# First stage of an attention block on one core: the depthwise convolution's input as four-row stacks read straight from memory, the value of two images in one column tile, results in 8 KB runs

## The chip, the core and the metric

The program runs on one core of a Trainium2 chip. The core has five engines with their own instruction streams: TensorE (PE, matrix products into PSUM), VectorE (DVE), ScalarE (ACT), GpSimd (POOL) and SyncE (SP, which here only issues transfers). Sixteen DMA engines move data; transfers are issued on a queue of SP, of ACT or of POOL. The metric is the device time of one execution in microseconds; the number quoted is the median of several.

## The reference, cut to what matters

Four layers follow one another on an input of 8 images, 384 channels, 32 x 32 pixels, all in float32. The change concerns only the first part of the first layer.

```python
def _bn(x, g, b):
    m = x.mean(axis=(0, 2, 3), keepdims=True)
    v = x.var(axis=(0, 2, 3), keepdims=True)
    return (x - m) * lax.rsqrt(v + EPS) * g[None, :, None, None] + b[None, :, None, None]

def _dwproj(x, dw, g, b, pw):
    C = x.shape[1]
    y = lax.conv_general_dilated(x, dw, (1, 1), ((1, 1), (1, 1)), feature_group_count=C, ...)
    y = jax.nn.gelu(_bn(y, g, b), approximate=False)
    return jnp.einsum('oc,bchw->bohw', pw, y)
...
q = _dwproj(x, dw_q, g_q, b_q, pw_q).reshape(B, heads, hd, N)
k = _dwproj(x, dw_k, g_k, b_k, pw_k).reshape(B, heads, hd, N)
v = _dwproj(x, dw_v, g_v, b_v, pw_v).reshape(B, heads, hd, N)
attn = jax.nn.softmax(jnp.einsum('bhcn,bhcm->bhnm', q, k) * scale, axis=-1)
```

Ahead of each layer the input is group-normed (12 channels a group). So the first stage computes, for each image, the group norm of x and then three depthwise 3 x 3 convolutions (q, k, v) with zero padding. The batch norm behind them takes its mean and variance over all images, so no attention can start before the convolutions of all eight images have been made and measured.

## The kernel before

The 384 channels are laid out as 128 partitions of 3 chunks (channel 3p + c is chunk c of partition p). An image has 1024 pixels, held as even rows and odd rows, 512 each (`HALF`).

The first stage (`pa`, up to line 534) works in four rounds of two images. The list `PLAN` gives each round eleven work units, each of which fills four PSUM banks and is then handled alike: ACT copies the banks to a result tile `y` (line 502; four such buffers), DVE takes the statistics of its four banks (line 504), and four DMAs, one for each quarter of 32 partitions, store it to DRAM. PE runs in 32 x 32 tiles, sixteen at a time: the row group is a quarter of the channels, the column group `q` one of two images times even or odd rows.

- A `u` unit convolves chunk 2 for one of q, k, v with nine taps from the normed image `xn`, with diagonal 32 x 32 weights `cwd`: 144 matmuls. Its results go by SP to `rawu`.
- An `s` unit takes chunk 0 or 1 of 32 channels from a stack tile `stk`, in which eight channels and four neighbouring rows share 32 partitions. Three taps along the row suffice, since the weights `cws` hold the three taps across rows. The 32 columns are q and k for even and odd outputs, or v with half of the columns unused: 48 matmuls for a pair. Its results go by POOL to `raws`.

The stack tiles are built from the normed image by `stack` (line 384): eight DMAs a tile on SP, with the four row offsets going to every fourth partition.

`norm(k)` makes the group norm of round k: DVE statistics of the two images (line 310), a matmul with `g4` that averages over the group, a second one for the spread of the means, a power on POOL for the inverse root (line 96), and the application by ACT (line 350), for one of the first two images by DVE (line 348), into a new tile `xn` with even and odd rows apart. `todo` puts the steps of round k + 1 among the units of round k. Images are loaded by `load_x`, the first on SP and ACT, the others on POOL.

With the last units, `spread_stacked` and `spread_scale` turn the statistics into scale and shift (through the matmuls `pmove` and `pfs`), and `gelu_image` applies them to q and k of image 0, which `load_b(0)` has fetched back. The scale of v comes last, at line 534. Then the attention stage begins (`pb`): its first matmul is the projection `pq` at line 638, and a memset of the value tiles `vt` (line 586) that stands behind the last scale. The order of instructions on each engine is set by a scheduler, from the order of the program text and the data that each needs.

Of the kernel before, what the change touches and what calls it, by code (L numbers as in the profile page):

```python
# [14 lines left out]
P = 128  # L15
# [6 lines left out]
NSTK = 4  # L22
# [31 lines left out]
def tile_kernel(ctx: ExitStack, tc: tile.TileContext, i: dict, out: bass.AP):  # L54
# [157 lines left out]
    raws = dram.tile([B, 2, 2, 16, 32, HALF], F32, name="raws")  # L212
    rawu = dram.tile([B, 3, 2, P, HALF], F32, name="rawu")
# [5 lines left out]
    def fetch_raw(g, v, rs, ru):  # L219

        for c in range(KC - 1):
            for e in range(2):
                k = 16 * (v % 2) + 8 * e
                nc.sync.dma_start(
                    out=g[:, c, e * HALF : (e + 1) * HALF], in_=rs[c, v // 2, :, k : k + 8, :]
                )
        nc.sync.dma_start(
            out=g[:, KC - 1, :].rearrange("p (e n) -> p e n", e=2),
            in_=ru.rearrange("e p n -> p e n"),
        )  # L230

    def load_b(b):
        acts[b] = {}
        for v in (2, 1, 0):
            acts[b][v] = image(f"g{v}_{b}")
            fetch_raw(acts[b][v], v, raws[b], rawu[b, v])
# [19 lines left out]
    with ExitStack() as pa:  # L256
        wa = pa.enter_context(tc.tile_pool(name="a_w", bufs=1))
        xa = pa.enter_context(tc.tile_pool(name="a_x", bufs=4))
        ya = pa.enter_context(tc.tile_pool(name="a_y", bufs=4))
        sa = pa.enter_context(tc.tile_pool(name="a_s", bufs=2))  # L260

        NK = B // 2
        last = NK - 1
        xts, xns = {}, {}

        def load_x(b, queue):
            xts[b] = image(f"xa{b}")
            load_image(xts[b], x_img[b], queue)

        load_x(0, nc.sync)  # L270
        load_x(1, nc.scalar)
        stk = [wa.tile([P, 2, 2, HALF], F32, name=f"stk{s}") for s in range(NSTK)]
        for t in stk:
            nc.gpsimd.memset(t, 0.0)
        g4 = const.tile([P, P], F32, name="g4_sb")
        nc.gpsimd.dma_start(out=g4, in_=i["g4"])
        cwd = wa.tile([P, 3, 9, 32], F32, name="cwd_sb")
        nc.gpsimd.dma_start(out=cwd, in_=i["cwd"])
        cws = wa.tile([P, 2, 4, 2, 3, 32], F32, name="cws_sb")
        nc.gpsimd.dma_start(out=cws, in_=i["cws"])  # L280
        ident = const.tile([P, P], F32, name="ident_sb")
        sels = wa.tile([P, P], F32, name="sels_sb")
        isv = wa.tile([P, 3], F32, name="isv_sb")
        msk = wa.tile([P, 16], F32, name="msk_sb")
        quad = wa.tile([P, 32], F32, name="quad_sb")

        def load_late():
            for t, nm in (
                (ident, "ident"), (sels, "sels"), (isv, "isv"), (msk, "msk"), (quad, "quad"),
                (gb0, "gb0"), *zip(w_in, ("wq0", "wk0", "wv0")),  # L290
            ):
                nc.gpsimd.dma_start(out=t, in_=i[nm])

        sst = wa.tile([P, 2, 16, NK, 6], F32, name="sst")
        smv = wa.tile([P, 2, 16, 2], F32, name="smv")
        fss = wa.tile([P, 3, 2, 2], F32, name="fss")
        cst = wa.tile([P, 3, 4, NK, 6], F32, name="cst")
        zmv = wa.tile([P, 3, 2, 4], F32, name="zmv")

        def norm(k):  # L300

            xt, state = [xts.pop(2 * k + j) for j in range(2)], {}
            st = sa.tile([P, 2, 2 * KC, 6], F32, tag="gp_st", name=f"gst{k}")
            mv = sa.tile([P, 2, 2], F32, tag="gp_mv", name=f"gmv{k}")
            xns[k] = [xa.tile([P, KC, N], F32, tag="xn", name=f"xn{k}_{j}") for j in range(2)]

            def begin(j):
                for m in range(2 * KC):
                    c, h = divmod(m, 2)
                    nc.vector.bn_stats(st[:, j, m, :], xt[j][:, c, h * HALF : (h + 1) * HALF])  # L310
                nc.vector.bn_aggr(mv[:, j, :], st[:, j].rearrange("p a b -> p (a b)"))

            def middle():
                pg = bank(f"gpa{k}")
                nc.tensor.matmul(
                    pg[:, 0:4], lhsT=g4, rhs=mv.rearrange("p j s -> p (j s)"),
                    start=True, stop=True,
                )
                ga = sa.tile([P, 2, 2], F32, tag="gp_ga", name=f"gga{k}")
                nc.vector.tensor_copy(ga.rearrange("p j s -> p (j s)"), pg[:, 0:4])  # L320
                dm = sa.tile([P, 2], F32, tag="gp_dm", name=f"gdm{k}")
                nc.vector.tensor_tensor(dm, mv[:, :, 0], ga[:, :, 0], ALU.subtract)
# [3 lines left out]
            def end():  # L326
                ga, dm = state["ga"], state["dm"]
                pb = bank(f"gpb{k}")
                nc.tensor.matmul(pb[:, 0:2], lhsT=g4, rhs=dm, start=True, stop=True)
                ve = sa.tile([P, 2], F32, tag="gp_ve", name=f"gve{k}")  # L330
                nc.vector.scalar_tensor_tensor(
                    ve, pb[:, 0:2], 1e-5, ga[:, :, 1], ALU.add, ALU.add
                )
                ss = sa.tile([P, 2, 2], F32, tag="gp_ss", name=f"gss{k}")
                rsqrt(ss[:, 0, :], ve, 2)
# [5 lines left out]
            def apply(c):  # L341
                ss = state["ss"]
                for j in range(2):
                    d = rows_of(xns[k][j][:, c, :], 0, H)
                    x = xt[j][:, c, :].rearrange("p (h e w) -> p h e w", e=2, w=W)
                    sc, sh = ss[:, 0, j : j + 1], ss[:, 1, j : j + 1]
                    if k == 0 and j == 1:
                        nc.vector.tensor_scalar(d, x, sc, sh, ALU.mult, ALU.add)
# [100 lines left out]
        for f in norm(0):  # L449
            f()  # L450
        normed.add(0)
        quads = [slice(32 * r, 32 * r + 32) for r in range(4)]
        for n, (k, kind, g, c) in enumerate(work):
            for k2, f in todo.get(n, ()):
                if f == 0:
                    steps[k2] = norm(k2)
# [1608 lines left out]
```

## Time and profile before

| | us |
|---|---|
| median of 3 runs | 3612.69 |
| lowest and highest | 3610.12, 3613.4 |
| the profiled execution | 3622.18 |
| its span, from the first to the last instruction | 3620.4 |
| PE busy | 3456.4 (95%) |
| DVE busy | 1664.5 (46%) |
| ACT busy | 1285.1 (35%) |
| POOL busy | 271.6 (8%) |
| mean granted TensorE clock | 0.979 |

The page gives busy time of each engine, a row of forty equal slices (a digit is tenths of the slice), DMA queues, the chain of work that ended last, and groups of equal instructions with the idle time ahead of them and what ended it. Other views of the trace list groups, waits or a timeline of a window, or give busy time, granted clock, DMA share and GB/s for stretches chosen by the reader. In a line of stretches the columns are: stretch, its length, busy time and instruction count of PE, PE's weight loads, DVE, ACT and POOL, then clock, DMA share and GB/s. A matmul of float32 leaves two records in the trace. The page's first slice covers 90.5 us, so the first stage takes nearly four slices.

### The profile page before, as it was taken

To read this page: it belongs to the slowest core of one execution; us is meant where nothing else is said; L and a number is where in the kernel's file an instruction comes from. 1 tells how busy PE (TensorE), PEld (TensorE's weight loads), DVE (VectorE), ACT (ScalarE), POOL (GpSimd) and SP (SyncE) were. 2 spreads that over 40 slices of the span, in tenths; PEclk is the share of its full clock that TensorE was granted. 3 is DMA by queue.
4 is the path that set the end of the run, shared out by engine and by line. 5 is a ranking of instruction groups with operands and counts; after the bars stand their busy time and mean duration, and the time that the engine had idled before them with its cause. 6 is when DMAs were issued, how large, how long until landed. Compare 5 with 4: busy or idle time off the path is not lost.

```text
span 3620.4 us, 50244 instructions
## 1 busy us (share of the span) xinstructions
PE 3456.4 (95%) x21323; PEld 1535.1 (42%) x21323; DVE 1664.5 (46%) x2766; ACT 1285.1 (35%) x1517; POOL 271.6 (8%) x310
## 2 busy tenths in 40 slices
PE   5877999999999999999899999999999999999897
PEld 3545343434343434344344534444344444444433
DVE  6434223232323232333346566465764647556663
ACT  3333444444454444444212331323322232322222
POOL 4212000000000000000000010200102010010112
PEclk9988999999999999999999999999999999999898
DMA  8785112121212121211521110110101001010000
GB/s 301 199 228 150 41 48 73 31 77 26 76 26 76 27 75 36 66 49 57 220 110 41 34 38 21 48 38 34 38 34 50 24 34 45 26 53 20 0 34 20
DMA packets 98151, 237.58 MB, mean 66 GB/s; under 512 B 16648, under 2 KB 20984, under 8 KB 97658
## 3 DMA queue, kind: packets, MB, share of 16 engines
q1 hardware_dynamic: 84954, 193.23, 16.9%
q0 software_dynamic: 11664, 37.84, 3.6%
q8 instruction: 172, 2.82, 0.3%
q10 hardware_dynamic: 1296, 3.15, 0.2%
q14 instruction: 65, 0.53, 0.0%
HBM read 132.89 MB, written 75.59 MB: 58 GB/s over the span
## 4 chain that ended last, share of the span: by engine, by line
PE 40%; DVE 9%; ACT 1%; DMA 1%; POOL 0%; issue 0%; DVEq 0%; ACTq 0%; POOLq 0%
PE y L1405 12%; PE ph L1384 9%; DVE y L1480 5%; PE pq L1525 3%; PE pw L1488 3%; PE pf L1832 3%; PE s L1703 2%; PE pav L1729 2%; DVE hd L1370 1%; DMA o<-o 1%; PE pk L1678 1%; PE pv L1687 1%; PE xsb L1664 1%; PE plog L1134 1%; PE pss L1742 1%; DVE off L1595 1%
## 5 line engine op out<-in xcount | busy, mean ns | idle before, releaser
L731 ACT ACTIVATE p<-s 128x1024 f32<-128x1024 f32 x512 | 497.0, 1022 | 365.2 <-PE s L724 364.7
L739 PE MATMUL pav<-p,vt 64*64 64x512 f32 x4096 | 494.4, 588 | 0.0
L1405 PE MATMUL y<-hd,w_sb 128*128 128x512 f32 x1080 | 488.7, 600 | 3.5 <-DVE hd L1370 3.5
L1384 PE MATMUL ph<-h,w_sb 128*128 128x512 f32 x1104 | 486.8, 595 | 5.0 <-ACT h L1333 5.0
L724 PE MATMUL s<-qk,qk 48*64 48x512 f32 x3072 | 370.5, 592 | 0.0
L1384 PEld LDWEIGHTS ph<-h,w_sb 128*128 128x128 f32 x1104 | 207.0, 190 | 266.2 <-issue 250.0
L1405 PEld LDWEIGHTS y<-hd,w_sb 128*128 128x128 f32 x1080 | 199.9, 191 | 248.2 <-issue 235.6
L739 PEld LDWEIGHTS pav<-p,vt 64*64 64x64 f32 x4096 | 167.4, 133 | 274.7 <-issue 274.3
L700 DVE COPY ta<-pav 128x512 f32<-128x512 f32 (+1 forms) x65 | 44.3, 682 | 475.2 <-PE pav L739 475.2
L1480 DVE SCALAR_TENSOR_TENSOR y<-h,tap,y 128x961 f32<-128x961 f32 (+1 forms) x192 | 235.0, 1250 | 0.6
L1394 ACT ACTIVATE hd<-ph,b_sb 128x512 f32<-128x512 f32 x180 | 122.9, 683 | 312.2 <-PE ph L1384 312.2
L1595 DVE SCALAR_TENSOR_TENSOR off<-q,dw_sb,off 128x225 f32<-128x225 f32 (+3 forms) x432 | 212.7, 552 | 1.6
L724 PEld LDWEIGHTS s<-qk,qk 48*64 48x64 f32 x3072 | 113.0, 133 | 221.2 <-issue 198.7
L492 PE MATMUL pk<-xn,cwd_sb 32*32 32x496 f32 (+3 forms) x3456 | 138.3, 632 | 29.2 <-issue 17.3
L502 ACT COPY y<-pk 128x1024 f32<-128x1024 f32 (+1 forms) x132 | 87.1, 740 | 193.6 <-issue 73.7
L1720 ACT ACTIVATE p<-s 128x1024 f32<-128x1024 f32 x96 | 96.2, 1024 | 166.4 <-PE s L1703 142.2
L79 DVE COPY qk<-pq 128x512 f32<-128x512 f32 x48 | 33.2, 692 | 262.0 <-PE pq L638 262.0
L1370 DVE TENSOR_TENSOR hd<-hd,cb 128x512 f32<-128x512 f32 x180 | 123.5, 691 | 40.9 <-ACT hd L1394 40.7
L492 PE MATMUL pk<-stk,cws_sb 32*32 32x496 f32 (+1 forms) x3072 | 124.9, 629 | 17.5 <-issue 11.4
L1765 POOL TENSOR_TENSOR p<-p,p 128x1024 f32<-128x1024 f32 x48 | 113.0, 2355 | 349.6 <-ACT p L1720 349.6
L1488 PE MATMUL pw<-y,upw 128*128 128x512 f32 x288 | 129.6, 603 | 4.4 <-DVE y L1480 4.4
L638 PE MATMUL pq<-g,wq_sb 128*128 128x512 f32 x288 | 130.3, 603 | 0.0
(306 smaller groups left out, 3910.3 us busy)
## 6 DMA issues: line engine op xcount, KB each, us to landing
g<-raws SPq DMA_DIRECT2D x96, 256.0 KB
raws<-y POOLq DMA_DIRECT2D x64, 256.0 KB, 6.9
rawu<-y SPq DMA_DIRECT2D x48, 256.0 KB
g<-rawu SPq DMA_DIRECT2D x24, 512.0 KB
xh<-in_x_dram SPq DMA_DIRECT2D x48, 256.0 KB
f<-in_x_dram SPq DMA_DIRECT2D x24, 512.0 KB
f<-o SPq DMA_DIRECT2D x24, 512.0 KB
o<-ot SPq DMA_DIRECT2D x42, 256.0 KB
```

Of the source, the lines that this page charges most:

```text
L492: nc.tensor.matmul(to[:, r0:r1, c0:c1], lhsT=cwd[rs, g, t, :] if kind == "u" else cws[rs, c, g, e, t, :], rhs=src[rs, r0 + d : r1 + d, c0 ...
L638: nc.tensor.matmul(pq, lhsT=w_in[v][:, c, pr * P : (pr + 1) * P], rhs=rows_of(acts[b][v][:, c, :], h * H // 2, (h + 1) * H // 2) if v == 0 ...
L724: nc.tensor.matmul(s[64 * k : 64 * k + 64, j * HALF : (j + 1) * HALF], lhsT=kt[r, k0 : k0 + 64], rhs=qt[r, h * HALF : (h + 1) * HALF], sta ...
L731: nc.scalar.activation(p, s, AF.Exp, scale=scale)
L739: nc.tensor.matmul(pav[k][64 * j : 64 * j + 64, :], lhsT=vts[b % 2][r, kc, 2 * hd : 2 * hd + 2, :].rearrange("p a b -> p (a b)"), rhs=p[r, ...
L1370: nc.vector.tensor_tensor(hd, hd, state["cb"], ALU.mult)
L1384: nc.tensor.matmul(ph, lhsT=w1[:, e, c, dc * P : (dc + 1) * P], rhs=state["h1"][c], start=(c == 0), stop=(c == KC - 1),)
L1394: nc.scalar.activation(hd, ph, AF.Relu, bias=b1[:, k : k + 1])
L1405: nc.tensor.matmul(y, lhsT=w2[:, e, dc, m * P : (m + 1) * P], rhs=state[h, k], start=(k == 0), stop=(k == NE * KC - 1),)
L1480: nc.vector.scalar_tensor_tensor(d, f, tap2[:, c, t : t + 1], d, ALU.mult, ALU.add)
L1488: nc.tensor.matmul(pw[h], lhsT=upw2[:, c, m * P : (m + 1) * P], rhs=y[c][:, hs], start=(c == 0), stop=(c == KC - 1),)
L1595: nc.vector.scalar_tensor_tensor(d, f, dw3[:, t : t + 1], d, ALU.mult, ALU.add)
```

## The change

- The input comes as a second DRAM array, `xs`, whose layout on the host keeps even and odd rows of each channel apart and has one row of zeros at either end. From it `load_half` reads tiles of four-row stacks of all three chunks: a tile holds half an image, that is two of the four groups of 32 channels, in each chunk, and comes in four DMAs (one a row offset) of 32 partitions, each partition a run of 12 KB. Two neighbouring row offsets of a stack come from the same memory shifted by one image row, so each row is read twice. There are sixteen such tiles, the first four loaded on SP and ACT, all others on SP, in pieces spread over the work units.
- `norm(k)` takes its statistics from the stacks (24 for two images, where there were 12) with a mask `gs4` that counts each row once, and applies scale and shift in place; POOL then multiplies the first and last row of each piece by 0 or 1 (`mrow`), since the padding must stay zero.
- The units: six `a` units a round (q and k, one chunk and two groups of 32 channels, two images: 48 matmuls), and three `v` units (one chunk, all groups), in which two images share one column tile: six passes, three an image, with the weights of the other image's columns zero (96 matmuls).
- Results go by SP to `rqk` and `rv` in an order that makes each partition's run 8 KB. `fetch_raw` reads them back in six DMAs a tensor instead of five.
- The moments of x that the attention stage needs (`xmv`) are made from the stack statistics, which `x_moments` first moves with eight DMAs of 24-byte runs.
- Scale and shift of q and k are made in the last round after its sixth unit (`spread_qk`), those of v at the end (`spread_v`).
- In this stage the engines keep the order of the program text (`manual_schedule`).

The diff, cut:

```diff
-    raws = dram.tile([B, 2, 2, 16, 32, HALF], F32, name="raws")
-    rawu = dram.tile([B, 3, 2, P, HALF], F32, name="rawu")
+    rqk = dram.tile([B, KC, 32, 16, HALF], F32, name="rqk")
+    rv = dram.tile([KC, B, 16, 16, HALF], F32, name="rv")
...
+            src = rw[c, 8 * e : 8 * e + 8] if v == 2 else rq[c, 16 * v + 8 * e :][:8]
+            nc.sync.dma_start(
+                out=g[:, c, e * HALF : (e + 1) * HALF], in_=src.rearrange("q a n -> a q n")
+            )
...
-        xa = pa.enter_context(tc.tile_pool(name="a_x", bufs=4))
+        xa = pa.enter_context(tc.tile_pool(name="a_x", bufs=6))
...
+        pa.enter_context(tc.manual_schedule(engines=set(ENGINES)))
...
+        IN_IM = (0, 1, 2, 3, 4, 11, 12)
+
+        def load_half(m, queue):
+            b, h = divmod(m, 2)
+            t = (
+                image(f"xs{m}") if m in IN_IM
+                else xa.tile([P, KC, N], F32, tag="xs", name=f"xs{m}")
+            )
...
+            def part(d):
+                w = KC * N
+                s = W + (0 if d in (1, 2) else W if d == 3 else -W)
+                src = i["xs"][s : s + B * C * N].rearrange("(b e m n) -> b e m n", b=B, e=2, m=32)
+                queue.dma_start(
+                    out=t.rearrange("p c n -> p (c n)")[d::4],
+                    in_=src[b, 1 - d % 2, :, h * w : (h + 1) * w],
+                )
...
+        for m in range(4):
+            for f in load_half(m, (nc.sync, nc.scalar)[m % 2]):
+                f()
...
+            def begin(j, h):
+                for g in (2 * h, 2 * h + 1):
+                    for c in range(KC):
+                        nc.vector.bn_stats(
+                            xst[:, g, 2 * k + j, c, :], xt[j][h][:, g % 2 * KC + c, :]
+                        )
...
+            def apply(g):
+                ss, h = state["ss"], g // 2
                 for j in range(2):
...
+                    d = xt[j][h][:, g % 2 * KC : g % 2 * KC + KC, :]
...
                     if k == 0 and j == 1:
+                        nc.vector.tensor_scalar(d, d, sc, sh, ALU.mult, ALU.add)
                     else:
+                        nc.scalar.activation(d, d, AF.Identity, bias=sh, scale=sc)
+                    for e, row in enumerate((0, HALF - W)):
+                        f = d[:, :, row : row + W]
+                        nc.gpsimd.tensor_tensor(
+                            f, f, mrow[:, e : e + 1].unsqueeze(2).to_broadcast([P, KC, W]),
+                            ALU.mult,
+                        )
...
-            "s00 s01 s10 u0 s11 s20 s21 u1 s30 s31 u2",
+        PLAN = ["a00 a10 v0 a01 a11 v1 a02 a12 v2"] * last + ["a00 a10 a01 a11 a02 a12 v0 v1 v2"]
...
+        AT = (0, 0, 1, 2, 3, 4, 5, 6, 7, 8), (0, 3, 3, 4, 5, 6, 6, 7, 7, 8)
...
+        def x_moments():
+            for g in range(4):
+                for e in range(2):
+                    nc.sync.dma_start(
+                        out=xnst.rearrange("p b c e s -> p (b c) e s")[32 * g : 32 * g + 32, :, e],
+                        in_=xst[e + 1 :: 4, g].rearrange("p b c s -> p (b c) s"),
+                    )
...
+            if at == 0:
+                for m in ((8, 9, 10, 11), (12,), (13, 14, 15), ())[k]:
+                    loads += load_half(m, nc.sync)
...
+                for a, f in zip(AT[k + 2 > last], norm(k + 1) if k < last else ()):
+                    steps.setdefault(a, []).append(f)
+            for _ in range(2 if k == 0 else 4):
+                if loads and (k > 0 or at > 1):
+                    loads.pop(0)()
...
+            passes = [(j, x) for j in range(2 if kind == "v" else 1) for x in (1, 0, 2)]
...
+                    if kind == "v":
+                        g, w = q, slice(48 - 16 * j, 80 - 16 * j)
                     else:
+                        (u, j), w = divmod(q, 2), slice(0, 32)
+                        g = 2 * s + u
+                    src = halves_of[4 * k + 2 * j + g // 2][:, g % 2 * KC + c, :]
...
                         nc.tensor.matmul(
+                            banks[r][quads[q]].rearrange("p (h w) -> p h w", w=W)[:, :, c0:c1],
+                            lhsT=cws[rs, c, g, x, w], rhs=src[rs, :, c0 + x - 1 : c1 + x - 1],
+                            start=(p == passes[0]), stop=(p == passes[-1]),
                         )
...
+                    nc.sync.dma_start(
+                        out=rqk[2 * k + j, c, :, 4 * g : 4 * g + 4, :], in_=y[quads[q]]
                     )
...
+        spread_v()
+        scales = scale_of(2, fv)
```

## The prediction

> **What bounds the kernel now.** I read the page's slices first, then the windows around the seam between the first stage and the attention stage, then groups, waits and the timeline at that seam.
>
> ```profile
> PE   5877999999999999999899999999999999999897
> PEclk9988999999999999999999999999999999999898
> DMA  8785112121212121211521110110101001010000
> ...
> 0.00:348.66 348.66, 252.79 (x6563) 157.27 (x6564) 157.45 (x355) 120.56 (x161) 96.11 (x172) 0.90 0.77 223
> 348.66:1700.00 1351.34, 1351.34 (x9154) 540.69 (x9158) 411.43 (x674) 640.95 (x654) 8.29 (x5) 1.00 0.19 53
> ```
>
> TensorE (PE) is busy 1351.34 of 1351.34 us after the seam, with no gap in which lost or won time could hide: what the first stage saves, the kernel saves. Only its 348.66 us, with PE busy 252.79, are in play. Two more answers say what fills them.
>
> ```profile
> 99.15:108.57 9.42, 9.42 (x289) 6.40 (x275) 7.11 (x12) 5.91 (x8) 3.09 (x6) 1.00 0.77 169
> ...
> 44.00:60.00 16.00, 6.84 (x162) 2.79 (x144) 14.47 (x31) 2.71 (x5) 5.58 (x11) 0.91 1.02 373
> ...
> 100.00:200.00 100.00, 80.55 (x2163) 49.91 (x2139) 40.59 (x71) 39.25 (x56) 26.03 (x49) 0.91 0.82 214
> ...
> 322.50:326.00 3.50, 3.30 (x98) 1.95 (x76) 3.43 (x12) 2.25 (x5) 1.00 (x2) 1.00 1.00 239
> ...
> L492 PE MATMUL pk<-xn,cwd_sb 32*32 32x496 f32 (+3 forms) x3456 | 138.3, 632 | 29.2 <-issue 17.3 <-ACT y L502 8.9 <-ACT xn L350 3.0
> L492 PE MATMUL pk<-stk,cws_sb 32*32 32x496 f32 (+1 forms) x3072 | 124.9, 629 | 17.5 <-issue 11.4 <-ACT y L502 6.1
> ...
> L504 DVE BATCH_NORM_STATS2 sst<-y 128x6 f32<-128x512 f32 x128 | 78.1, 679 | 54.9 <-ACT y L502 54.7
> ...
> ACT y L502 <- DMA rawu<-y: 49.5, 4, 17.8
> ```
>
> See four things. First, 99.15 to 108.57 is three undisturbed stacked units (96 records each, two per matmul): 3.14 us a unit, 32.7 ns a record. All 6528 records at that rate are 213 us; the rest is waiting. Second, the longest single cause named is ACT's copy waiting for the result buffer `y` until its store has left (49.5 us in 4 waits). Third, DMA: 373 GB/s in 44 to 60, where loads dominate, but 214 over 100 to 200. Fourth, 322.50 to 326.00 is a window where only result stores run, from the SP queue, with all engines full (1.00) at 239 GB/s. So a store out of a 32-partition quarter of `y` runs at 239 GB/s, a load at nearer 400.
>
> **The change part by part.**
>
> PE. Nine-tap chunk-2 units (432 matmuls a round) and stacked units (384) become six q/k units of 48 and three value units of 96: 576 against 816, in four rounds 4608 records against 6528. At 32.7 ns: 151 us of PE instead of 213. At the slower rate of the last nine-tap units (11.14 us between the copies that start at 308.44 and 319.58, for 288 records: 38.7 ns) the value half would add 14 us. The zero columns that let two images share a value tile cost nothing[...]. From the scale matmul on, PE's instruction order is the same in both programs.
>
> DVE. A round has 36 statistics of `y` (44 before) and 24 of the input (12 before), since each row stands in two stack partitions: 60 at 0.68 us plus 8 aggregates at about 0.3 are 43 us a round. Four rounds less the first input, read before PE starts, are 154; with the last round's aggregates (36 x 0.22 and 24 x 0.19, 12.5), four applies of 1.2 and some 3 for the scale steps, DVE needs about 175 us after PE's start: longer than PE.
>
> ACT. Copies are 2 us a unit, 72 in all. The norm in place is 28 activations of 128x1536; from 1.24 us for 128x1024 in the row of L350, 1.85 each, 52 us. With two GELU images, 131 us: covered by DVE's 175. If an apply waits for its scale, the copies queued behind it on ACT wait, and PE with them; two units of PSUM absorb some 6 us.
>
> POOL. It loses 128 result issues and 7 us of memsets and gains 64 edge-row multiplications of 128x96. From 0.557 us at 128x144 and 0.707 at 128x192 (the `wt` multiplications), a straight line gives 0.41 each, 26 us in all, beside other work except the first. Its power of 8 columns takes 1.64 us (row of `rs`) instead of 0.72.
>
> DMA and queues. Gone: 128 stacking copies (16 MB, 0.61 us of SP each). The input is read twice over: 25.2 MB against 12.6, in 12 KB rows. Results stay 37.7 MB, but all 144 stores now go through SP beside the loads, the fetch of image 0 (18 DMAs, 4.7 MB) and eight small copies of 24-byte runs, and in the program's order each waits for the DMA eight before it on the SP and ACT queues. Two hundred issues at up to 0.69 us (median of `rawu`) are 140 us of SP: covered.
>
> Store price: 37.7 MB at the trace's 239 GB/s are 158 us, 4.4 us a unit. The Trainium skill (SBUF — State Buffer, Door 1: the DMA port swizzle) says that DMA speed follows the number of the 16 ports that a transfer's partitions reach; 32 consecutive partitions reach 8, half of its 435 GB/s, 218. That gives 173 us. I take the row, 158; longer runs do not lift a port limit.
>
> Load price: the skill speaks against these loads (DMA: Bandwidth & Descriptors, Rules for kernel authors): for full bandwidth, 128 partitions and 1 MiB per DMA; here it is 32 and 384 KB. The trace has stacking copies of 120 to 128 KB into the same every-fourth partitions inside the 409 GB/s of 44 to 54, and 378 GB/s for the first 512 KB loads (2 to 12). I take 390; by the rule's side I price the loads like stores, 239. Half of them, 12.6 MB, fall behind PE's start: 32 us, or 53.
>
> The 24-byte copies have no near row. Below nothing is excluded, for they add work; 6144 runs at 11 ns (the packets of 48 B) over 16 engines are 4 us. Dearer by six, 24 us. I take 4, nearest to that row.
>
> Start. Before, PE starts at 19.9 us. Now four half-image tiles (6.3 MB) and 1.5 MB of weights must land: at 378 GB/s, at 22.7. The last two tiles come together: 12 statistics and 4 aggregates, 9 us, to 31.7; the scale chain 3.6 + 0.9, to 36; first apply and edge rows 2.6: PE at about 39. That is 19 us lost. By then the other four tiles are in too (14.1 MB in all, 36 us at 390).
>
> Sum after the start, for DMA: late weights 5, stores 158, loads 32, image 0 at 380 GB/s 12, runs 4: 211 us, plus 3 idle before the first store: the last store lands at 253. The end does not wait for that: of four `y` buffers one is the scratch tile of the scale step, so three units of stores (13 us) are still under way at the last copy: 240. DVE alone would give 39 + 175 = 214. DMA binds, by 26 us. Part of the loads should ride beside stores[...]; I give that 8 us: 232. Then statistics, aggregates, scale matmul as before (346.5 to 348.7), 2.2: the seam is at 234.
>
> Before it was 348.7: 115 us won. Given back: the memset of the value tiles waits for the last stores (245), takes 7, and values can be copied from 252.6; before, 15.4 us after the seam (364.1), now 18.4: 3 us, some under score matmuls. And the late scale (AT puts it two units later in round 2): 2. Net 110.
>
> The profiled execution took 3622.18 us (span 3620.4 and 1.8 around it): 3512. The median of the runs shown is 9.5 us lower; the same saving from 3612.7 is **3503**.
>
> **The rivals.**
>
> *Loads hide under stores* (0.16). Then DVE binds: 214, seam 216, and some 130 us are won: about 3483. For it: the 409 GB/s where reading and writing mix.[...]
>
> *Loads are slow too, or the one queue stutters* (0.25). At 239 GB/s for every load, 21 us more behind the start, and 10 before it; with the mixed 214 of 100 to 200 us, all 55 MB take 257. The win is 47 to 79: about 3548. For it: SP waits for each unit's copy before it can issue later loads.
>
> *The queue becomes slower than PE was* (0.07), the other side: about 202 DMAs stand behind the start on SP, eight at a time. If the mean from issue to landing is L, they need 202 L / 8. L = 12.3 us makes 310, and the seam is where it was; each microsecond more costs 25. At L = 13, near 3632. The page's 6.9 us for results, 8.4 at the median for loads, 15.3 at most, speak against it, not decisively. The small copies could add to it, since the stores of the last round stand behind them.
>
> *It does not do what it says*: the order lists 576 matmuls a round, no stacking copies, and 12 KB and 8 KB rows. Excluded but for the rates.
>
> **How the numbers follow.** The reckoned case has 0.50 (3488 to 3520), the two faster rivals 0.41, slower 0.07, 0.02 in between. Range 3478 to 3560: it holds the first three but for their tails. A difference under 0.2% (7 us) could not be told from none here. Faster 0.91, same 0.02, slower 0.07.
>
> **What would show it.** PE's first convolution near 39; 4608 records; store-only stretches at 220 to 240 GB/s with DMA share near 1; ACT's copies waiting for DMA of `rqk`/`rv` from the second round; the first query projection near 234 to 240; then the same 1.00 busy. DVE without gaps and no such waits: the first rival. DMA share well under 1 while PE waits: the second or third. I am wrong if the seam lies past 300, or the stage after it has gaps.

## The result, and the profile after

The changed kernel takes 3549.4 us (median of 4 runs, 3546.18 to 3553.0); before takes 3613.05 beside it. The ratio is 0.9822, with a 95% interval of 0.9805 to 0.9839: 63.7 us won. The forecast was 3503, with a range of 3478 to 3560: the direction is right, the gain is little more than half of the 110 us reckoned.

Profile against profile, 3622.18 us became 3547.47: 74.7 us won. That is more than between the medians, since the profiled execution of before stood 9.1 us above its median and that of after 1.9 below. The prediction's working is compared with the profiles in what follows.

The page's slices, as they were shown of before:

```profile
PE   4789999999999999998999999999999999999898
PEclk9989999999999999999999999999999999999898
DMA  8883212121212121111700110100101011110000
```

And the two windows on either side of the first query projection `pq`:

```profile
0.00:276.59 276.59, 189.45 (x4628) 104.59 (x4629) 168.40 (x379) 124.16 (x144) 38.30 (x88) 0.91 0.82 258
276.59:1628.00 1351.41, 1351.41 (x9163) 541.72 (x9167) 411.63 (x675) 641.63 (x655) 8.29 (x5) 1.00 0.20 56
```

`pq` starts at 276.59 us instead of 348.88. Behind it PE is busy without a gap, and what is left of the span is 3268.8 us against 3271.5. So 72.3 of the span's 75.0 us lie ahead of that seam, as the prediction said they would; but the seam was to be at 234. All that follows is about these 43 us.

In the first 276.59 us PE is busy 189, DVE 168 and ACT 124, and the mean DMA share is 0.82. No resource is full. The costliest groups of the first stage:

```profile
L514 PE MATMUL pk<-xs,cws_sb 32*32 32x496 f32 (+1 forms) x4608 | 185.0, 650 | 35.6 <-issue 20.9 <-ACT y L524 5.7 <-POOL xs L380 5.5
L332 DVE BATCH_NORM_STATS2 xst<-xs 128x6 f32<-128x512 f32 x96 | 59.0, 670 | 12.9 <-DMA xs<-in_xs_dram 12.9
L527 DVE BATCH_NORM_STATS2 sqk<-y 128x6 f32<-128x512 f32 x96 | 58.7, 675 | 38.9 <-ACT y L524 38.9
```

And its waits from 38 us on, when PE starts on the convolutions (who <- for whom: us in total, times, longest):

```profile
ACT y L524 <- PE pk L514: 66.1, 13, 14.8
...
PE pk L514 <- issue: 20.9, 14, 2.9
...
ACT y L524 <- DMA rqk<-y: 12.7, 2, 6.4
PE gpa L341 <- DVE gmv L335: 12.2, 3, 5.9
```

The matmul records are the 4608 expected. ACT waits for the stores of q and k only 12.7 us, in two waits, and 3.0 for one of v (before: 49.5 in four, and 12.3); it waits 66.1 us for PE. And PE waits for `gpa`, the first matmul of the input norm, which needs the input statistics `gmv` of DVE. From 38 us to the seam, 238.6 us, PE is busy 188.2 and stands still 50.4: 20.9 on "issue", when it waits for nothing that the profile shows (the last section comes back to this), 12.2 at `gpa`, the rest in small pieces. The rounds, cut up, show where this happens (columns: stretch, length, busy PE, weight loads, DVE, ACT, POOL, then clock, DMA share, GB/s):

```profile
38.00:98.00 60.00, 50.30 (x1226) 27.85 (x1231) 37.14 (x71) 32.62 (x36) 16.51 (x40) 0.94 0.76 244
98.00:130.00 32.00, 19.95 (x443) 8.76 (x419) 27.45 (x55) 8.36 (x13) 0.00 (x0) 0.84 0.78 257
130.00:157.00 27.00, 24.71 (x730) 15.02 (x731) 11.79 (x22) 22.11 (x24) 6.84 (x17) 1.00 0.79 189
157.00:206.00 49.00, 35.21 (x833) 17.02 (x836) 31.90 (x62) 12.16 (x19) 1.09 (x1) 0.83 0.86 279
206.00:225.00 19.00, 16.45 (x388) 8.68 (x366) 6.08 (x11) 18.22 (x17) 5.74 (x17) 0.91 0.92 259
225.00:276.00 51.00, 41.12 (x1056) 25.72 (x1054) 33.29 (x119) 25.97 (x35) 1.70 (x2) 0.90 0.80 207
```

Round 1 is 98 to 157. In its first 32 us DVE is busy 27.45 and ACT 8.36; in its last 27 us ACT is busy 22.11 and DVE 11.79. Each engine has work for half a round, and not at the same time. The timeline of DVE in the first part of round 1 says what the work is:

```profile
99.90 1.86 DVE L332 BATCH_NORM_STATS2 xst<-xs 128x6 f32<-128x512 f32 x3
101.80 0.24 DVE L335 BATCH_NORM_AGGREGATE gmv<-xst 128x2 f32<-128x18 f32 x1
101.95 1.81 DVE L332 BATCH_NORM_STATS2 xst<-xs 128x6 f32<-128x512 f32 x3
103.80 0.24 DVE L335 BATCH_NORM_AGGREGATE gmv<-xst 128x2 f32<-128x18 f32 x1
...
108.05 2.41 DVE L527 BATCH_NORM_STATS2 sqk<-y 128x6 f32<-128x512 f32 x4
```

Half an image costs DVE 4.1 us (first four lines). Four such steps, `begin` in the diff, stand at the head of rounds 0 and 1, two of them ahead of the first unit's own statistics; in round 2 one stands at the head and three behind the value unit. DVE's order is fixed, so in round 1 it works without a gap from 97.5 to 123.7, through these four steps and the statistics of four units, the first of them round 0's last. PE's order is fixed too: it cannot pass `gpa` before all four are done, and so has made only three units by then.

```profile
121.03 0.58 PE L341 MATMUL gpa<-gmv,gs_sb 128*128 128x16 f32 x2 [3.61 <-DVE gmv L335]
```

The wait of 3.6 us is the smaller part: PE had also lost 6.4 us on "issue" in 98 to 130, and the clock granted there is 0.84. Behind `gpa` comes a serial chain, here in round 2 (the timeline of all engines, cut to the chain):

```profile
191.08 0.58 PE L341 MATMUL gpa<-gmv,gs_sb 128*128 128x16 f32 x2 [5.94 <-DVE gmv L335]
...
191.59 10.03 PE L514 MATMUL pk<-xs,cws_sb 32*32 32x512 f32 x192
...
202.25 0.39 PE L356 MATMUL gpb<-gdm,gs_sb 128*128 128x8 f32 x2 [0.62 <-ACT y L524]
...
204.91 1.64 POOL L98 TENSOR_TENSOR gss<-gve,mhalf 128x8 f32<-128x8 f32 x1 [49.08 <-DVE gve L358]
...
206.78 1.67 ACT L377 ACTIVATE xs<-xs,gss 128x1536 f32<-128x1536 f32 x1 [3.12 <-DVE gss L363]
```

PE stands 5.9 us at `gpa`; the value unit behind it, 192 records or 6.3 us at the undisturbed rate, takes 10.0; `gpb`, the power and the first apply follow, and the applies then lie between the copies on ACT until 223.

### The profile page after: what moved, and what is told of

It is laid out like the page before. It is cut to its first block, busy times and chain, and to the rows that moved or that the text cites. A ratio compares the mean times of both kernels' runs of the same rounds, so it can differ in the third digit from the quotient of the medians.

```text
span 3545.4 us, 46334 instructions
## 1 busy us (share of the span) xinstructions
PE 3393.4 (96%) x19381; PEld 1484.0 (42%) x19381; DVE 1676.0 (47%) x2791; ACT 1287.1 (36%) x1500; POOL 213.7 (6%) x226
## 4 chain that ended last, share of the span: by engine, by line
PE 40%; DVE 9%; DMA 1%; ACT 1%; POOL 1%; issue 0%; DVEq 0%; ACTq 0%; POOLq 0%
PE y L1428 12%; PE ph L1407 9%; DVE y L1503 5%; PE pq L1548 3%; PE pw L1511 3%; PE pf L1855 3%; PE s L1726 2%; PE pav L1752 2%; DVE hd L1393 1%; DMA o<-o 1%; PE pk L1701 1%; PE pv L1710 1%; PE xsb L1687 1%; PE pss L1765 1%; PE plog L1157 1%; DVE off L1618 1%
## 5 line engine op out<-in xcount | busy, mean ns | idle before, releaser
L514 PE MATMUL pk<-xs,cws_sb 32*32 32x496 f32 (+1 forms) x4608 | 185.0, 650 | 35.6 <-issue 20.9
L514 PEld LDWEIGHTS pk<-xs,cws_sb 32*32 32x32 f32 x4608 | 100.4, 108 | 111.9 <-issue 59.4
L660 PE MATMUL pq<-g,wk_sb 128*128 128x512 f32 x288 | 129.2, 598 | 0.0
```

The lines of the kernel that those rows point to most:

```text
L514: nc.tensor.matmul(banks[r][quads[q]].rearrange("p (h w) -> p h w", w=W)[:, :, c0:c1], lhsT=cws[rs, c, g, x, w], rhs=src[rs, :, c0 + x - 1 ...
L660: nc.tensor.matmul(pq, lhsT=w_in[v][:, c, pr * P : (pr + 1) * P], rhs=rows_of(acts[b][v][:, c, :], h * H // 2, (h + 1) * H // 2) if v == 0 ...
```

## The experiments

Every row is one kernel; the diffs are against the changed kernel, and shortened. Round lengths are the distances between the ends of ACT's last copies, taken from the trace, round 0 from 38 us on. "Rest" is the span less the start of `pq`. It is 3268 to 3272 us in every run but those of the slow stores, so the `pq` column, from one profiled execution each, is the finer measure, and the ratio to before on the same chip the one with an interval. The ratios carry a difference of their own: the medians of before were 3616 to 3622 us beside the experiments and 3613 beside the changed kernel, so two ratios can differ by 0.1 to 0.2% (3 to 8 us) without a cause in the edit. The medians themselves lie 10 us under the changed kernel's for e1, 15 for e2 and 11 for e3, which is nearer to `pq`.

| run | rounds 0, 1, 2, 3 | `pq` | rest | median | ratio to before, 95% |
|---|---|---|---|---|---|
| changed kernel | 60.4, 58.7, 67.8, 49.1 | 276.6 | 3268.8 | 3549.4 | 0.9822 (0.9805-0.9839) |
| e1 one store a unit | 58.6, 62.0, 62.5, 46.7 | 270.4 | 3270.9 | 3539.3 | 0.9778 (0.9758-0.9798) |
| e2 a third of the input statistics | 52.6, 53.0, 64.7, 49.3 | 260.2 | 3269.0 | 3534.8 | 0.9770 (0.9752-0.9789) |
| e3 statistics early | 57.7, 56.7, 65.6, 47.3 | 267.7 | 3270.8 | 3538.5 | 0.9779 (0.9760-0.9797) |
| e4 runs of 2 KB | 59.7, 60.6, 64.9, 49.1 | 274.7 | 3268.2 | 3547.7 | 0.9803 (0.9780-0.9826) |
| e5 half of the applies on DVE | 57.8, 58.6, 62.5, 54.2 | 273.5 | 3270.0 | 3545.7 | 0.9799 (0.9783-0.9815) |
| e6 `gpb` behind `gpa` | 61.1, 57.2, 64.5, 50.3 | 273.5 | 3268.2 | 3542.7 | 0.9790 (0.9774-0.9806) |
| e7 two wide stores | 113, 163, 161, 197 | 674.4 | 3286.6 | 3958.6 | 1.0939 (1.0921-1.0958) |
| e8 all with wide stores | 114, 155, 160, 198 | 668.0 | 3282.2 | 3952.9 | 1.0928 (1.0909-1.0946) |
| e9 three orders | 57.4, 54.7, 62.9, 56.1 | 271.6 | 3270.2 | 3543.6 | 0.9782 (0.9765-0.9798) |
| e10 e9, one store a unit | 56.3, 55.3, 55.9, 52.5 | 260.5 | 3268.5 | 3530.8 | 0.9748 (0.9732-0.9765) |
| e11 value by image | 63.6, 64.8, 68.1, 51.7 | 289.3 | 3271.5 | 3559.2 | 0.9824 (0.9807-0.9841) |
| e12 e9, wide stores by 64 rows | 58.4, 54.4, 60.9, 58.3 | 272.5 | 3269.5 | 3543.8 | 0.9795 (0.9781-0.9808) |

e4, which left all engines' work alone, moved the rounds by 0.7, 1.9, 2.9 and 0 us: so much two profiles can differ.

**e1: are the stores the bound?**

```diff
-            for q in range(4): ... four stores of y[quads[q]]
+            nc.sync.dma_start(out=dst, in_=y)   # dst: 1 MB in one piece
```

> Each unit's four stores (32 partitions each, in 8 KB runs) become one store of all 128 partitions to one contiguous megabyte; the results lie in another order in memory, so the later stages work on permuted values of the same kind. Theory DMA (the prediction's: stores of 32 partitions at 239 GB/s in one queue bind the first stage): the price of a store falls to that of a load, some 9 us a round come off, the first scale matmul after the first stage moves from 276 to about 235 and the time falls to about 3510 us. Theory DVE (the input statistics of the next round stand ahead of the units' own statistics in VectorE's order and pace the front half of each round): DMA had room, so only the last round's waits of ScalarE for stores (12.7 us in two) can go; the matmul moves to 264-276, the time is 3537 to 3550 us.

`pq` came 6.2 us earlier, at 270.4. Theory DMA wanted about 235. The DMA share from 38 us to the seam fell from 0.81 to 0.71, so the transfers were relieved. But the stores as the change has them are worth 6 us, not 41; they do not bind rounds 0 and 1, which moved by -1.8 and +3.3. What was won lies in round 2 (5.3) and round 3 (2.4).

**e2: is it the input statistics?**

```diff
-                    for c in range(KC):
+                    for c in range(KC if k == 0 else 1):
                         nc.vector.bn_stats(...)
+                    # k > 0: entries 1 and 2 copied from entry 0
```

> For rounds 1 to 3 the input statistics are taken of one chunk of three (the other two entries are copies of the first), so the scales are of a third of the data; all else is as in the changed kernel. VectorE loses about 9 us of work in the front half of rounds 0, 1 and 2. Theory DVE: each of these rounds gets shorter by 7 to 9 us, the first scale matmul moves from 276 to about 250, the time is about 3524 us. Theory DMA: VectorE is not the bound, the matmul stays within 5 us of 276, the time within 3544 to 3552 us. Theory ACT (the applies and copies on ScalarE pace the rounds): as theory DMA.

`pq` came 16.4 us earlier, and no run is within 9 us of the changed kernel's fastest. By round:

```profile
38.00:90.00 52.00, 44.72 (x1216) 26.43 (x1224) 29.67 (x63) 32.70 (x37) 16.70 (x41) 1.00 0.83 278
90.00:143.00 53.00, 46.79 (x1212) 26.79 (x1189) 31.03 (x67) 30.08 (x37) 6.83 (x17) 0.94 0.85 252
143.00:208.00 65.00, 48.38 (x1163) 24.39 (x1156) 30.14 (x65) 30.35 (x36) 6.84 (x17) 0.89 0.93 287
208.00:259.00 51.00, 42.61 (x1058) 24.89 (x1054) 33.20 (x117) 26.43 (x36) 1.70 (x2) 0.90 0.79 207
```

Rounds 0 and 1 shrank by 7.8 and 5.7 us, against the 8 us of work taken out of each front half (a half image costs 2.1 us instead of 4.1, four times). Round 2 gave 3.1 of the 7 to 9 expected, with the DMA share at 0.93: there something else was next. So theory DVE holds for two rounds of three, and theories DMA and ACT, which expected nothing, fall for these. It explains 16 of the 43 us, not all.

**e3: same work, spread; the loads for round 2 come earlier, too.**

```diff
-        AT = (0, 0, 1, 2, 3, 4, 5, 6, 7, 8), (0, 3, 3, 4, 5, 6, 6, 7, 7, 8)
+        AT = {1: (0, 0, 1, 2, 3, 4, 5, 6, 7, 8),     # unit of the whole list
+              2: (5, 6, 7, 10, 11, 12, 13, 14, 15, 16),
+              3: (13, 21, 21, 22, 23, 24, 24, 25, 25, 26)}
```

> Same work, other order: the loads for round 2 that need no buffer of round 0 come in round 0's first three units, and three of the four input statistics of round 2 are taken in the back half of round 0 (units 5 to 7), where VectorE idled for 12 of 27 us; the first of round 3 is taken in the back half of round 1. Round 1's front half then has one such step in place of four, round 2's three in place of four. Theory DVE: round 1 gets 10 to 13 us shorter, round 2 about 3, round 0 up to 4 longer: 3537 to 3542 us. Theory DMA: nothing is taken off the transfers, and the early loads stand in front of round 0's stores: 3548 to 3556 us. Theory order (the wait of TensorE for the spread of the statistics, wherever these were taken, costs the time): at most 3 us less.

`pq` at 267.7, 8.9 us earlier, and 11 by the medians. Most of the gain was expected in round 1, which got only 2.0 shorter; the rest came in pieces of about 2 us from the other rounds, no larger than two profiles can differ, so where it comes from is not shown. The waits of rounds 1 and 2 show what held round 1:

```profile
PE gpa L346 <- DVE gmv L340: 22.0, 2, 12.9
DVE xst L337 <- DMA xs<-in_xs_dram: 9.9, 2, 8.2
```

Three of four statistics were done early, but the fourth half needs a buffer of round 0, arrived at 107.8 us, and DVE, with the units behind it, waited 8.2 us for it; PE waited 12.9 at `gpa`. A statistic placed ahead of its data held up all that stood behind it. This is the fastest version with all results in their places. (The expectation's "idled for 12 of 27 us" has the numbers turned round: in 130 to 157 DVE is busy 11.8 us and idle 15.)

**e4: back to runs of 2 KB.**

```diff
-    rqk = dram.tile([B, KC, 32, 16, HALF], ...)
+    rqk = dram.tile([B, KC, 16, 32, HALF], ...)
```

> The results go back to runs of 2 KB (row-slice ahead of channel in memory), the rest of the change stands; stores and fetches have the same bytes with four times the runs. Theory DMA: stores get dearer or stay as they are, and what they lose comes onto the first stage's end one to one: 3550 to 3580 us. Theory DVE: DMA has 12 to 24 per cent of room in each round, so at most 5 us come on: 3547 to 3555 us.

`pq` at 274.7, median 3547.7: no difference that these runs can show. The 8 KB runs, one of the change's three parts, show no worth in this place. (The fallback of the attention stage is not adapted to this layout; it does not run on these inputs.)

**e5 and e6: two links of the chain.**

```diff
-                    if k == 0 and j == 1:          # e5: apply on DVE
+                    if j == 1:
-        AT = (0, 0, 1, 2, 3, 4, ...), (0, 3, 3, 4, 5, 6, ...)   # e6
+        AT = (0, 0, 1, 2, 3, 3, ...), (0, 3, 3, 4, 5, 5, ...)
```

> The applies of each second image (4 a round) run on VectorE (1.09 us each) in place of ScalarE (1.68 us). Theory chain (in the back half of a round the applies and copies of ScalarE pace the units, 22 of 27 us, while VectorE idles for 12): each of rounds 0, 1 and 2 gets 4 to 6 us shorter, the first scale matmul after the first stage moves from 276 to about 262, the time falls to about 3535 us. Theory totals (VectorE's sum of work over the stage is the bound, wherever it lies): 13 us of VectorE's work come on, the matmul moves to 280-289, the time is 3553 to 3562 us.

> The second matmul of the input norm (gpb) is put directly behind the first (gpa), with no unit between: one unit earlier in each of rounds 0 to 2; the applies keep their places. Theory chain (round 2 is paced by the arrival of its last half, its statistics, gpa, a unit at the low clock of 8 to 9 us, gpb, the power and eight applies, one after the other): that unit leaves the chain, round 2 gets about 8 us shorter, rounds 0 and 1 by 0 to 3; the time is 3536 to 3541 us. Theory totals or theory ACT (the applies and copies on ScalarE need their time anyway): within 3 us of 3549.

Each moved `pq` by 3.1 us, to 273.5: a fifth (e5) and two fifths (e6) of what theory chain expected, but against theory totals too, by which e5 should have been slower. In the back half of round 1 of e5 two units fell from 5 us to 3.4, but the last rose from 5 to 6; rounds 0 to 2 together got 8.1 us shorter, and round 3 longer by 5.1. In e6 round 2 lost 3.3 us, hardly more than two profiles differ, and the others moved within that. e5 is the first sign of a second bound: time won in rounds 0 to 2 was taken back in round 3.

**e7 and e8: wider stores that were slower.**

```diff
+    for u in range(2):        # q and k; a unit of v by one store in three dimensions
+        nc.sync.dma_start(out=rqk[2*k : 2*k+2, c, :, 4*g : 4*g+4]   # 2 x 32 x 8 KB
+            .rearrange("j q a n -> j q (a n)"), in_=flat[64*u : 64*u+64])
```

> Same results in the same places, by fewer and wider stores: two of 64 partitions for a unit of q and k, one of 128 partitions for a unit of v, in place of four of 32. Theory chain: as the single store to a contiguous megabyte did, some 5 to 12 us come off, mostly by SP's issues and the last round: 3537 to 3544 us. Theory DMA for the rest of the time: if it was the contiguous megabyte that helped, not the width, nothing comes off: 3547 to 3552 us.

> Together: applies of the second image on VectorE, gpb directly behind gpa, wide stores, and the early input statistics with round 2's chain put two units later than in the earlier trial (its last half landed at 107.8 us and TensorE waited 12.9 us for gpa there). Theory chain: gains of 14, 8, 7 and 15 us that overlap in part; rounds of 50 to 54 us, the scale matmul at 235 to 245, the time 3505 to 3520 us. Theory totals (VectorE 188 us of work from 38 on is a floor of 226, reached only without a gap): not under 3530 us, since the moved applies make VectorE dearer.

Both theories missed: 409 us slower than the changed kernel. A unit of q and k takes about 21 us. The slices of DMA in e7 from 200 to 300 us:

```profile
DMA  1111116611111122223111111111111111121122
GB/s 82 52 57 52 52 54 193 195 52 52 59 52 59 52 70 87 98 102 121 72 52 52 52 52 59 52 59 54 54 52 59 59 52 52 53 66 52 52 85 69
```

A flat 52 GB/s with a share of about an eighth: as two of sixteen engines would give it. The packets of 8 KB took 309 ns (median) in these 100 us by the trace, 26.5 GB/s, and twice that is about the 52. Counted from the trace, exactly two packets are under way for 69% of the 100 us. The outer dimension of the transfer is 2 (two images), and by this it seems to be dealt out; e12 puts that to the test. e8, with the same stores, tells nothing about the orders. (The 188 us in its expectation are PE's in 38 to 276, not DVE's, which are 148.)

**e9 and e10: the orders alone, and with the stores relieved.**

```diff
+        AT = {1: (0, 0, 1, 2, 3, 3, 5, 6, 7, 8),
+              2: (5, 6, 7, 12, 13, 13, 14, 15, 16, 17),
+              3: (15, 21, 21, 22, 23, 23, 24, 25, 25, 26)}    # with e5's applies
```

> The three orders together, with the stores as the change has them (four of 32 partitions): early input statistics with round 2's chain two units later than in the first trial, gpb directly behind gpa, applies of the second image on VectorE. Theory chain (serial norm chain and uneven VectorE set the pace): the single gains of the scale matmul, 9, 3.5 and 3.5 us, and up to 10 for the 12.9 us wait for gpa that the later place removes: the matmul at 250 to 260, the time 3522 to 3535 us. Theory DMA next (once the rounds are shorter, stores and loads fill the engines, and round 3 gives it back, as the trial with applies on VectorE did with 5 us): the matmul at 264 to 270, the time 3538 to 3543 us.

> As the three orders together, and each unit stored by one DMA of 128 partitions to one contiguous megabyte (results in another order in memory, the later stages work on permuted values). Theory chain: stores are worth 6 us of the matmul as they were alone, or less: 0 to 6 us under the run of the three orders. Theory DMA next: with the norm chain out of the way the transfers bind, and relief of them is worth more than alone: 12 to 25 us under it, the matmul at 240 or earlier.

e9: rounds 0 to 2 are together 11.9 us shorter than in the changed kernel, round 3 is 7.0 longer, and `pq` is at 271.6. Single gains of 8.9, 3.1 and 3.1 came to 5.0, so theory DMA next is nearer (its 264 to 270 was still too early). In round 3 of e9 ACT waits for stores:

```profile
ACT y L534 <- DMA rqk<-y: 15.3, 2, 8.9
```

That is only 2.6 more than the changed kernel's 12.7, which also lie in its round 3, so it does not account for the 7.0 us that round 3 became longer; what does is not shown.

e10 relieves the stores: 11.1 us under e9, where the same relief alone (e1) had given 6.2. Relief of the transfers is worth more once the norm chain is shorter. The gain is a near miss (12 to 25 expected), the seam a clear one (240 or earlier expected). And most of the gain is not in round 3: round 2 got 7.0 us shorter, round 3 got 3.6. The DMA row of the changed kernel from 236 to 259 us, in round 3:

```profile
DMA packets 2651, 5.82 MB, mean 253 GB/s; under 512 B 1948, under 2 KB 1948, under 8 KB 1948
```

And that of e10 from 223 to 236 us, in round 3:

```profile
DMA packets 987, 5.09 MB, mean 392 GB/s; under 512 B 109, under 2 KB 109, under 8 KB 454
```

So stores of 32 partitions do run at about 250 GB/s (with few other bytes: of the 2651 packets 1948 are the small copies), and a store of all 128 at 392. In the last round, where there is no norm, ACT waits for them; but relief of 10.2 of these 12.7 us (e1, where 2.5 are left) shortened the round by 2.4 only.

**e11: the value of each image in its own unit again.**

```diff
-  "a00 a10 v0 a01 a11 v1 a02 a12 v2"                 # w = slice(48 - 16*j, 80 - 16*j)
+  "a00 a10 v00 v01 a01 a11 v10 v11 a02 a12 v20 v21"  # w = slice(48, 80)
```

> One part of the change undone: each image's value has its own column tile and unit again (three passes of 48 matmuls, 12 units a round in place of 9, stores of 16 partitions); bytes and matmuls are the same. Three more units a round cost VectorE 3 x 2.45 us of statistics and ScalarE 3 x 1.9 us of copies. Theory chain (VectorE's work paces): 5 to 10 us come on to each round, the scale matmul at 296 to 316, the time 3569 to 3590 us. Theory DMA: bytes are the same, the matmul at 276 to 282, the time 3549 to 3556 us, unless stores of 16 partitions are slow.

`pq` at 289.3: 12.7 us later. Between the theories: neither nothing, nor 5 to 10 us a round (it was 3.2, 6.1, 0.3 and 2.6). DVE's statistics of `v` doubled (96 in place of 48, 58.1 us busy for 29.5), and ACT's copies took 95.4 us for 71.6; which part of this fell into idle time was not taken apart. The ratio shows nothing of these 13 us (0.9824 with an interval of 0.0034 about it), but the medians do: 3559.2 is 9.8 above the changed kernel, and e9, run beside it on the same chip, is 15.6 under it by the median and 17.7 by `pq`. So the pairing's worth is some 10 to 13 us by two measures, and nothing by the third.

**e12: wide stores with 64 rows outermost, loads first.**

```diff
-    rqk = dram.tile([B, KC, 32, 16, HALF], ...)
+    rqk2 = dram.tile([B // 2, KC, 2, 32, 16, HALF], ...)
+    ... out=rqk2[k, c].rearrange("j q a n -> (j q) a n")[:, 4*g : 4*g+4]
-            for _ in range(2 if k == 0 else 4):
+            for _ in range(12 if n == 18 else 4):
```

> The three orders together (early statistics, gpb behind gpa, applies of the second image on VectorE), and two more edits. The q and k results of two images lie next to each other in memory, so that a unit's two stores of 64 partitions each have one outer dimension of 64 rows in place of 2 times 32 (the fallback for softmax sums out of range, which does not run on these inputs, is not adapted to it); and round 2's three loads (halves 13 to 15) are all issued in its first unit, ahead of that unit's stores, in place of four a unit between them. If the two-store trial was slow because its transfer went by an outer dimension of 2, onto 2 of 16 engines, the stores now run at the full rate, some 8 us for all rows of a unit or less; if 64 partitions are slow by their width, it is 20 us a unit and about 3950 us again. Theory chain: round 2's wait for gpa (16.5 us for that unit) falls to about 8, the scale matmul is at 258 to 264, the time 3527 to 3533 us. Theory DMA next: wide stores and earlier loads relieve what round 3 gave back, two thirds of the 11 us that the single store was worth there: with the shorter wait the matmul at 252 to 258, the time 3521 to 3527 us.

The stores were no longer slow. The window of round 3 in which mostly they run:

```profile
242.00:253.00 11.00, 7.56 (x189) 4.97 (x179) 3.94 (x14) 3.32 (x5) 0.00 (x0) 0.81 1.00 339
```

All engines are full, at 339 GB/s, and by the trace 15 to 17 packets are under way for 90% of the window, so it was not the width that made e7 slow. What is left is its outer dimension of 2 (that the two images now lie next to each other in memory was not tried apart from it). But the time is that of e9: `pq` at 272.5, and both theories missed. Round 2's `gpa` came 34.4 us after the round began, as it did in the changed kernel (191.1 less 157.1 is 34.0), although the loads were issued ahead of all stores. What held it in e12 was first PE, then DVE:

```profile
157.75 4.43 PE L525 MATMUL pk<-xs,cws_sb 32*32 32x496 f32 x128 [1.32 <-issue]
164.22 4.40 PE L525 MATMUL pk<-xs,cws_sb 32*32 32x512 f32 x128 [2.04 <-issue]
170.69 4.38 PE L525 MATMUL pk<-xs,cws_sb 32*32 32x496 f32 x128 [2.07 <-issue]
...
185.16 0.58 PE L347 MATMUL gpa<-gmv,gs_sb 128*128 128x16 f32 x2 [7.25 <-DVE gmv L341]
```

PE works off 128 records (64 matmuls) in 4.4 us and then stands for 1.3 to 2.1 us with nothing to wait for that the profile shows. DVE's last three input steps stand behind the statistics of the value unit, which waits for PE; so DVE begins them at 170.4, is busy until they are done at 185.0, and PE stands 7.25 us at `gpa`. More on PE's stops below.

## Why the prediction was right or wrong, point by point

- *Only the first stage is in play, PE has no gap behind the seam.* Right: the rest of the span moved by 2.7 us. The 3 us charged to the memset of the value tiles did not show.
- *PE starts at about 39.* Right: 37.92. The price of loads was right too: the first 36 us ran at 350 to 480 GB/s after their start, 391 on the mean, so the prediction's estimate of 239 from the Trainium skill's rule of 128 partitions a transfer (DMA: Bandwidth & Descriptors, Rules for kernel authors) would have been too low.
- *4608 records, 151 us.* The count is right. Undisturbed (130 to 157) a record took 33.8 ns (24.71 us for 730), near the 32.7 reckoned. But in 98 to 130 it took 45 (19.95 us for 443), at a clock of 0.84, and right behind the wait at `gpa` in round 2 it took 52 (10.03 us for 192). Over 38 to 276 PE was busy 188, 37 us more than the term of 151.
- *DVE needs 175 us after the start, ACT 131.* Too high: 148 and 119, in part since four statistics in a row take 2.41 us, not four times 0.68, and an apply 1.68 in place of 1.85.
- *The store's price is 239 GB/s.* Right where it can be seen: 253 GB/s with little but stores in round 3, at a share of 0.92. The measured row was better than the 218 that the prediction worked out from the port rule.
- *DMA binds, 211 us after the start, and DVE alone would be done at 214.* **This is the step that failed**, in two ways. The DMA engines' share makes about 192 us of work in 38 to 276 (share times length, summed over the six windows above), 19 under the 211. And no total bound: e1 took the stores' price away and moved `pq` by 6 us, where the step wanted 41; e2 took 23 us of DVE's work away (147.7 to 124.6), from which by this step nothing should have come, and moved it by 16. A sum per resource, and then the largest, presumes that the others can run beside it at any time. Here the input norm is a chain through DVE, PE, POOL and ACT in a fixed order, DVE's part of it stands in the front half of each round and ACT's at its tail. Beside it PE itself, priced at 151 us, took 188 and stood still for another 50. The transfers had a part only in rounds 2 and 3 (e1: 5.3 and 2.4 us; e10 against e9: 7.0 and 3.6).
- *The late scale costs 2 us.* The same mistake in small: round 2, with the later places of `AT`, took 67.8 us against 58.7 of round 1. Part of these 9 us belongs to loads and the fetch of image 0, which also fall into it.
- *The 24-byte copies cost 4 us.* Their packets took 7 ns each (median of the 24-byte ones), not 11, but they held SP's queue for 7.6 us (228.6 to 236.3), with the DMA share at 0.44 in the second half of it. What of this reached the seam was not tried alone.
- *The rivals.* The time is that of the second rival (3548), and that is luck: its loads were not slow, the transfers ran at 240 GB/s on the mean and not at its 214, and no run shows that the one queue stuttered. That the time lies in the stated range is owed to this rival, not to the reckoned case. DVE as the bound, the first rival, was the right engine with the wrong form: not its total, but its place in each round. "If an apply waits for its scale, the copies queued behind it wait" stood in the prediction, and no term of the sum came from it.

What stays open: the reliefs tried together (e10) end at 260.5, not at 234. Its rounds are still 52 to 56 us, with PE busy 177 of 222 at clocks of 0.88 to 0.94, so PE's stops, its clock and the wait for round 3's norm (20 us between the copies of two units of round 2, 8.1 of them at `gpa`) share the remaining 26 us; they were not taken apart.

## What to carry to other kernels

When a stage shares its work among engines that run in a written-out order, do not take the largest of the totals for its length. Cut one round into its halves, ask for each half which engine has work in it, and follow the longest dependent chain (here statistics, matmul, matmul, power, apply) through it: here idle time in one half did not pay for work in the other. And after each bound that is relieved, look for where the next resource takes the time back; gains of 9, 3 and 3 us became 5 together.

## What the runs showed of the hardware that was not expected

**A transfer is dealt out by its outer dimension.** Two stores of 512 KB with an outer dimension of 2 ran at 52 GB/s, a share of an eighth, with two packets under way at a time (e7); the same bytes from the same 64 partitions with 64 rows outermost ran at up to 339, with 15 to 17 packets (e12). A unit of q and k took about 21 us instead of about 4. The number of engines is read from share, rate and the packets in flight; the trace does not name the engine of a packet.

**PE stops every 128 records while data fills the DMA engines.** The trace has another traffic than the data, here of the changed kernel from 38 to 276 us:

```profile
q1 hardware_dynamic: 17296, 54.43, 76.9%
...
q8 instruction: 36, 0.59, 1.0%
```

36 packets of 16 KB (0.59 MB by 36), and 36 times 128 is 4608, the number of convolution records in that stretch. In the changed kernel's quiet window, 130 to 157 us, PE's only stops of over 0.3 us behind its start at 130.5 come 128 records apart, for 0.4 to 0.7 us; in e12, with the loads in one go, the stops are 1.3 to 2.1 us of every 6.5. And they follow the packets: all 14 stops of the changed kernel's PE on "issue", 20.9 us together, end 1.31 to 1.47 us after a packet of this queue has landed. That PE's instructions come through the same DMA engines, beside the data, and PE stops when they are late fits all of this; no run took the fetches alone away, so it is argued, not shown. What the stops cost is open too. They come to 20.9 us in the changed kernel, 19.1 in e1, 14.0 in e2, 25.5 in e9 and 15.1 in e10, which does not simply follow the DMA share (0.81, 0.71, 0.86, 0.80 and 0.71), and a stop can be hidden where PE waits for something else anyway.
